# Two batches' adjacency patterns in one 32-bit word: a dilation ranked pair by pair in a two-layer graph network

## The chip, the cores and the metric

The kernel runs on one core of a Trainium2 chip. The metric is the device time of one execution in microseconds (us), from the first to the last instruction. The engines are named as in the profile: PE is TensorE's matmul, PEld its weight load, DVE is VectorE, ACT is ScalarE, POOL is GpSimd, and SP is the engine that issues most of the DMAs.

## The reference

The input is 16 graphs (batches) of 1024 nodes with 128 features (`x`), a weighted adjacency matrix `adj` of 1024 x 1024 for each (a fraction of about 0.06 of it is above zero, the pattern is symmetric), and a node mask of ones. Two layers are computed:

```
# layer 0
h = relu(layernorm(x))
three times:  h = h @ W + b;  nh = h / |h|;  h = (adj * (nh @ nh.T)) @ h     (relu after the last)
x = x + h
# layer 1
h = relu(layernorm(x))
keep = dilate(adj > 0)
three times:  agg = (adj * keep) @ h / degree;  out = agg @ Wr + h @ Wx + b
              h = batchnorm(relu(out / |out|))
x = x + concat(h1, h2, h3) @ Wl + bl
```

The dilation is the part that the change touches. It works on the true/false pattern of one batch, and it goes row by row, since what earlier rows remove is missing in later ones:

```
for n in range(1024):
    row  = pattern[n];  num = sum(row)
    sf   = (num + 1) // 2  if num > 10  else 1
    rank = cumsum(row)
    rm   = row & (rank % sf == 0)            # only where num > 1 and the mask is set
    pattern[n] = row & ~rm
    pattern[:, n] &= ~rm                     # the same entries in the column
```

So a row with more than 10 entries loses the entry of rank `sf`, and where `num` is even also the last one. For this, the rank of every entry in the row as it then stands is needed.

## The kernel before

Nodes lie in 8 chunks of 128, so that a 128 x 128 block of the adjacency is one tile. Layer 0 and the dilation don't depend on one another, and the kernel lays them side by side; layer 1 begins when both are done.

**Layer 0** (`layer0`, `Batch`) goes over 48 steps, 16 batches by 3 convolutions, two batches at a time in turn. In a step each of the 8 row chunks gets its products `pg` of normalised features (PE, L344), which DVE multiplies with the adjacency out of PSUM into `ew` (L353, L356). `pg` has two PSUM buffers. PE then turns part of `ew` (L373), ACT brings that back (`ew`, L374), and the sums go to `po` (L384, L398), which ACT evicts at the end of the step (`hTo`, L407). The sums of a row chunk are issued three chunks after its products. Some steps also turn a batch's adjacency on PE (`pt_a`, L260, evicted to `adjA`).

**The dilation** (`dilation`, `dilate`) goes over 16 blocks: 8 row chunks by 2 halves of 8 batches. The 128 nodes of a row chunk lie on the partitions. Of a block three generators are made.

- `loads()`, for each of 8 batches: 128 rows of the adjacency (`an`) are loaded by SP, ACT makes the pattern of ones and zeros in f16 with Sign and Relu (L587, L588; Relu counts the entries into `rest`), and DVE writes the part to the left of the diagonal block, times what was kept there by earlier rows (L594, with the count in `left`). That part comes through a transposing DMA from `keep_d`. After every fourth batch, PE transposes the four diagonal blocks (L608), ACT evicts them (`dT`, L610), and three matmuls each (L614 to L616) give `T`, the rank of every entry of the diagonal block counted from the row's middle (evicted by ACT, L618).
- `rounds()`: within a row chunk the rows depend on one another, and that is solved by iteration: 2 to 6 rounds of a guess `E` for the removed entries (DVE, L667) and its count on PE (`pc`, L673). Then `fin` holds, for each row, where the removed ranks lie.
- `scans()`: the removed entries of the diagonal block are subtracted from the pattern (DVE, L732). Then, for each of 8 batches, one running sum over the row of 1024 gives twice the rank, less one, of every entry (DVE, L741, `rank`); ACT takes the distance from the row's middle (Abs, L751); DVE compares with the radius (`kp`, L762), and POOL's queue stores `kp` to `keep_d` (L763).

The patterns of all blocks live in a ring `patt` of 10 slots; the pattern of batch `i` in a block is slot `(at0 + i) % SLOTS`. The next block's loads are taken one after each scan of the block before.

Where the rounds don't settle, where a row has 10 entries or fewer, or where a zero turns up that mustn't, a counter `astray` is raised, and a general loop (`dilation(exact=True)`, under `tc.If`) does the whole dilation again row by row.

**Order.** `dilation()` yields weights, an estimate of how much time a piece takes. After each piece, steps of layer 0 are issued until their share of the work has caught up:

```
total = 2 * (NCH * (BH * (0.75 + 3.3) + 0.4 + 2.5) + sum(ROUNDS) * 1.0)
for weight in dilation():
    done += weight
    while at * total < done * SPREAD * total0 and step0():
        pass
```

with `SPREAD` 0.93. Within this the framework's scheduler may place instructions of an engine a little earlier or later by priority; `tc.keep_in_program_order` holds the scans and the Abs in their order.

Of the kernel before, what the change touches and what calls it, by code (L numbers as in the profile page):

```python
# [8 lines left out]
F32 = mybir.dt.float32  # L9
F16 = mybir.dt.float16  # L10
I32 = mybir.dt.int32
AF = mybir.ActivationFunctionType
ALU = mybir.AluOpType
PSUM = bass.MemoryType.PSUM
# [2 lines left out]
P = 128  # L17
# [3 lines left out]
EVENS = 16777216.0  # L21

NEVER = -4096.0

LOW = 20.0

# [2 lines left out]
ROUNDS = (2, 2, 4, 6, 6, 3, 2, 6)  # L29
# [17 lines left out]
def tile_adj_preln_d2(  # L47
# [40 lines left out]
    nc = tc.nc  # L88
    B, N, D = x.shape
    NCH = N // P  # L90
# [4 lines left out]
    GT = 4  # L95
# [26 lines left out]
    ident16 = const.tile([P, P], F16, name="ident16")  # L122
# [36 lines left out]

    def transposed(psum_pool, dst, src, nm, func=AF.Copy, halves=range(NHALF)):  # L160

# [38 lines left out]
    with ExitStack() as actx:  # L200
        dctx = ExitStack()
        poold = dctx.enter_context(tc.tile_pool(name="ad", bufs=2, side="right"))
# [14 lines left out]
        off = pool1.tile([P, P], F16, name="off")  # L217
        after = pool1.tile([P, P], F16, name="after")
        for fill, value, op in ((0.0, -2.0, ALU.is_ge), (4.0 * FAR, 2.0 * FAR, ALU.is_gt)):
# [4 lines left out]
                up, up, pattern=[[1, P]], compare_op=op, fill=fill, base=0, channel_multiplier=-1  # L224
# [303 lines left out]

        BH = B // 2
        SLOTS = BH + 2  # L530
        patt = poold.tile([P, SLOTS, N + 2], F16, bufs=1, name="patt")
        nc.gpsimd.memset(patt[:, :, 0:2], 0.0)

        astray = poold.tile([P, BH], F32, bufs=1, name="astray")
        nc.vector.memset(astray, 0.0)
# [27 lines left out]
        def dilate(k, half, exact):  # L563

            nk = f"{'e' if exact else ''}{k}_{half}"
            cols = slice(k * P, (k + 1) * P)
            diag = slice(2 + k * P, 2 + (k + 1) * P)
            at0 = (2 * k + half) * BH

            def pattern(i):  # L570
                return patt[:, (at0 + i) % SLOTS, :]

            left = poold.tile([P, BH], F32, tag="left", name=f"left{nk}")
            rest = poold.tile([P, BH], F32, tag="rest", name=f"rest{nk}")
            if k == 0:
                nc.vector.memset(left, 0.0)
            rbias = poold.tile([P, BH], F32, tag="rbias", name=f"rbias{nk}")
            T = poold.tile([P, BH, P], F16, tag="T", name=f"T{nk}")
            E = radius = shift = low = None

            def loads():
                for i in range(BH):
                    b = half * BH + i
                    an = poold.tile([P, N], F32, tag="an", name=f"an{nk}_{i}")
                    nc.sync.dma_start(an, adj[b, cols, :])
                    on = pattern(i)[:, 2 + k * P :]
# [16 lines left out]
                    if i % GT == GT - 1:  # L603
                        four = range(i - GT + 1, i + 1)
                        bs_ = slice(i - GT + 1, i + 1)
                        pdt = ps_sm.tile([P, GT, P], F16, tag="sm", name=f"pdt{nk}_{i}")
                        for n, ii in enumerate(four):
                            nc.tensor.transpose(pdt[:, n, :], pattern(ii)[:, diag], ident16)  # L608
                        dT = poold.tile([P, GT, P], F16, tag="dT", bufs=1, name=f"dT{nk}_{i}")
                        nc.scalar.activation(dT, pdt, AF.Copy)  # L610
                        nc.vector.tensor_scalar(rbias[:, bs_], rest[:, bs_], 2.0, -2.0, ALU.mult, ALU.add)
                        pT = ps_sm.tile([P, GT, P], F32, tag="sm", name=f"pT{nk}_{i}")
                        for n, ii in enumerate(four):
                            nc.tensor.matmul(pT[:, n, :], lhsT=dT[:, n, :], rhs=upto, start=True, stop=False)  # L614
                            nc.tensor.matmul(pT[:, n, :], lhsT=pattern(ii)[:, diag], rhs=off, start=False, stop=False)
                            nc.tensor.matmul(pT[:, n, :], lhsT=ident16, rhs=after, start=False, stop=True)  # L616
                        for n, ii in enumerate(four):
                            nc.scalar.activation(T[:, ii, :], pT[:, n, :], AF.Identity, bias=rbias[:, ii : ii + 1])  # L618
                    yield 0.8

            def rounds():
                nonlocal E, radius, shift, low

                x0 = poold.tile([P, BH], F32, tag="x0", name=f"x0{nk}")
                nc.vector.scalar_tensor_tensor(x0, left, -0.5, rest, ALU.add, ALU.add)
                nc.vector.tensor_tensor(x0, x0, mbias[:, half * BH : (half + 1) * BH, k], ALU.add)
# [10 lines left out]
                E = poold.tile([P, BH, P], F16, tag="E", name=f"E{nk}")  # L637
# [87 lines left out]
            def scans():  # L725

                i = 0
                while i < BH:
                    at_ = (at0 + i) % SLOTS
                    n = min(BH - i, SLOTS - at_)  # L730
                    here = patt[:, at_ : at_ + n, diag]
                    nc.vector.tensor_tensor(here, here, E[:, i : i + n, :], ALU.subtract)  # L732
                    i += n
                ranks = {}
                for i in range(BH + 1):
                    if i < BH:

                        pt = pattern(i)
                        ranks[i] = rank = poold.tile([P, N], F16, tag="rank", bufs=3, name=f"rank{nk}_{i}")
                        tc.keep_in_program_order(  # L740
                            nc.vector.tensor_tensor_scan(rank, pt[:, 1 : N + 1], pt[:, 2:], 0.0, ALU.add, ALU.add)  # L741
                        )
                        yield True, 2.5
                    if i == 0:
                        continue

                    i -= 1
                    b = half * BH + i
                    pt, rank = pattern(i), ranks.pop(i)
                    tc.keep_in_program_order(  # L750
                        nc.scalar.activation(  # L751
                            rank, rank, AF.Abs, bias=shift[:, i : i + 1], scale=1.0 if exact else -1.0
                        )
                    )
                    kp = poold.tile([P, N], F16, tag="kp", name=f"kp{nk}_{i}")
                    if exact:
                        nc.vector.tensor_scalar(
                            kp, rank, low[:, i : i + 1], radius[:, i : i + 1], ALU.max, ALU.not_equal
                        )
                        nc.vector.tensor_tensor(kp, kp, pt[:, 2:], ALU.is_ge)  # L760
                    else:
                        nc.vector.tensor_scalar(kp, rank, radius[:, i : i + 1], None, ALU.not_equal)  # L762
                    nc.gpsimd.dma_start(keep_d[b][cols, :], kp)  # L763
                    yield False, 0.8

            return loads(), rounds(), scans()

# [71 lines left out]
    with ExitStack() as bctx:  # L839
# [135 lines left out]
        with kctx, ExitStack() as c1:  # L975
# [53 lines left out]
            for b in range(B):  # L1029
# [3 lines left out]
                now = Sums(0, b, hT, 3, 1, ps_a)  # L1033
# [76 lines left out]
        for l in (1, 2):  # L1110
            last = None
            then = start2(l, 0)
            for b in range(B):
                now, hT = then
# [23 lines left out]
            for h, pp, a in late:  # L1138
# [4 lines left out]
                for c in range(CPH):  # L1143
                    n = h * CPH + c
# [4 lines left out]
        for b in range(B):  # L1149
            y = pool2.tile([P, NCH, D], F32, tag=("o", "own")[b % 2], name=f"y_{b}")  # L1150
            for h, pp, a in project(2, b, normed(3, b, ab)):
                hc = slice(h * CPH, (h + 1) * CPH)

                if b % 2 == 0 and h == 1:
                    for c in range(CPH):
                        n = h * CPH + c
# [3 lines left out]
                for c in range(CPH):  # L1160
                    n = h * CPH + c
# [55 lines left out]
```

## Time and profile before

| | us |
|---|---|
| median of 3 runs | 2819.03 (2815.42 to 2820.99) |
| profiled execution, span | 2818.8 |
| PE busy | 2649.9 (94%) |
| DVE busy | 1947.1 (69%) |
| ACT busy | 1426.5 (51%) |
| POOL busy | 477.6 (17%) |
| 128 scans (L741) | 294.9, from 79.5 to 1511.1 us |

Busy time says how long an engine had an instruction in it; the matmuls overlap one another, and their ends are modelled. The page gives the span of the profiled execution and no other time for it. Layer 0 takes up to about 1640 us, the dilation ends at about 1515 us, and the convolutions of layer 1 take the rest. In a group's row there stand the line, the engine, the operation, what it writes and reads, the count, then busy us and mean ns of one, then the engine's idle time before these instructions and what ended it. In a row of waits there stand who waited for whom, the us in total, the times and the longest.

### The profile page before, as it was taken

The numbers are of one execution on the slowest core, as the hardware profiler recorded it, in microseconds if no ns is written. First come the engines' busy times: TensorE is split into PE (matmuls) and PEld (weight loads), VectorE is DVE, ScalarE is ACT, GpSimd is POOL, SyncE is SP. The second block draws the span as 40 slices with busy tenths as digits, with TensorE's granted clock in tenths as the row PEclk, the third lists the DMA queues.
The fourth block names the chain that finished last, engine by engine and source line by source line (L and its number), as shares of the span: only waits on it lengthen the run. The fifth ranks groups of instructions, "written<-read, shape, count | busy, mean of one in ns | idle before, by whom it ended". The sixth has DMA issues, their size and how long they took to land. (4 is left out here: it accounts for less than half of the span.)

```text
span 2818.8 us, 51980 instructions
## 1 busy us (share of the span) xinstructions
PE 2649.9 (94%) x18803; PEld 2193.2 (78%) x18803; DVE 1947.1 (69%) x4943; ACT 1426.5 (51%) x4097; POOL 477.6 (17%) x616
## 2 busy tenths in 40 slices
PE   6999999999999999999999999999989999999997
PEld 4666666676776676666676778888889999899997
DVE  3778778788888788889886467777762333456556
ACT  6757667558556566466454333343333334333334
POOL 3112112012012111121121012222220101010101
PEclk9999999999999999999999999999999999999999
DMA  8437347258366476386354069999976666576774
GB/s 283 135 128 241 99 159 240 75 159 245 85 201 173 101 226 186 95 254 182 93 178 162 1 234 386 402 402 387 402 297 214 203 216 201 188 238 228 234 237 135
DMA packets 382233, 585.22 MB, mean 208 GB/s; under 512 B 85200, under 2 KB 266448, under 8 KB 381968
## 3 DMA queue, kind: packets, MB, share of 16 engines
q1 hardware_dynamic: 343280, 425.28, 48.2%
q0 software_dynamic: 38688, 156.53, 14.8%
q8 instruction: 151, 2.47, 0.4%
q14 instruction: 114, 0.93, 0.1%
HBM read 403.44 MB, written 163.58 MB: 201 GB/s over the span
## 5 line engine op out<-in xcount | busy, mean ns | idle before, releaser
L890 PE MATMUL agg<-hw,aT 128*128 128x128 f32 (+1 forms) x6144 | 743.5, 277 | 8.2 <-DVE aT L995 7.3
L890 PEld LDWEIGHTS agg<-hw,aT 128*128 128x128 f32 x6144 | 713.4, 193 | 13.6 <-DVE aT L995 9.7
L344 PE MATMUL pg<-nhT 128*128 128x512 f32 (+3 forms) x1152 | 454.7, 497 | 40.4 <-DVE ew L356 39.1
L384 PE MATMUL po<-ew,hS 128*128 128x512 f32 (+3 forms) x1152 | 453.3, 497 | 8.1 <-ACT hTo L407 3.7
L356 DVE TENSOR_TENSOR ew<-pg,adjA 128x768 f32<-128x768 f32 (+3 forms) x528 | 423.6, 826 | 5.0 <-PE pg L344 5.0
L398 PEld LDWEIGHTS po<-ew,hS 128*128 128x128 f32 x2688 | 339.5, 193 | 39.1 <-issue 36.8
L398 PE MATMUL po<-ew,hS 128*128 128x128 f32 x2688 | 367.5, 277 | 1.2 <-ACT ew L374 1.2
L374 ACT ACTIVATE ew<-gt 128x512 f32<-128x512 f32 (+1 forms) x480 | 208.5, 464 | 245.3 <-PE gt L373 238.0
L741 DVE TENSOR_TENSOR_SCAN rank<-patt 128x1024 f16<-128x1024 f16 x128 | 294.9, 2305 | 0.1
L344 PEld LDWEIGHTS pg<-nhT 128*128 128x128 f32 x1152 | 187.9, 192 | 131.7 <-issue 89.3
L384 PEld LDWEIGHTS po<-ew,hS 128*128 128x128 f32 x1152 | 195.2, 193 | 99.8 <-issue 64.6
L373 PEld LDWEIGHTS gt<-ident,ew 128*128 128x128 f32 x1344 | 168.5, 143 | 100.7 <-issue 75.4
L373 PE MATMUL gt<-ident,ew 128*128 128x128 f32 x1344 | 212.3, 277 | 4.8 <-PEq L824 2.5
L948 POOL TENSOR_TENSOR o<-o,rn 128x512 f32<-128x512 f32 x93 | 108.5, 1167 | 638.3 <-DVE rn L942 627.6
L353 DVE TENSOR_TENSOR ew<-pg,adjA 128x128 f32<-128x128 f32 x384 | 108.1, 282 | 156.6 <-PE pg L344 117.3
L864 DVE TENSOR_TENSOR own<-pw,bs 128x256 f32<-128x256 f32 x192 | 81.4, 424 | 155.5 <-ACT hw L863 155.4
L862 PE MATMUL pw<-wrx,hT 128*128 128x256 f32 x768 | 179.7, 388 | 9.2 <-ACT hT L1065 8.4
L862 PEld LDWEIGHTS pw<-wrx,hT 128*128 128x128 f32 x768 | 145.1, 194 | 31.3 <-ACT hT L1065 9.2
L1013 ACT ACTIVATE aT<-pta 128x512 f32<-128x512 f32 (+3 forms) x160 | 71.3, 467 | 187.4 <-PE pta L1012 181.9
L751 ACT ACTIVATE rank<-rank,fin 128x1024 f16<-128x1024 f16 x128 | 146.7, 1151 | 36.3 <-DVE rank L741 35.6
L940 ACT ACTIVATE own<-o 128x128 f32<-128x128 f32 x378 | 112.7, 301 | 99.7 <-DVE o L919 99.5
L321 POOL TENSOR_TENSOR hS<-hN,rn 128x1024 f32<-128x1024 f32 x48 | 102.5, 2136 | 355.5 <-DVE rn L157 226.0
(169 smaller groups left out, 3930.6 us busy)
## 6 DMA issues: line engine op xcount, KB each, us to landing
an<-in_adj_dram SPq DMA_DIRECT2D x128, 512.0 KB, 4.3
keep<-kp POOLq DMA_DIRECT2D x128, 256.0 KB, 2.9
kb<-keep SPq DMA_DIRECT2D x128, 256.0 KB, 5.5
aT<-adT SPq DMA_DIRECT2D x32, 960.0 KB, 4.7
aT<-adT SPq DMA_DIRECT2D x32, 832.0 KB, 4.6
aT<-adT SPq DMA_DIRECT2D x32, 704.0 KB, 4.2
aT<-adT SPq DMA_DIRECT2D x32, 576.0 KB, 3.4
xb<-in_x_dram SPq DMA_DIRECT2D x31, 512.0 KB, 5.2
```

The costliest lines, as they stand in the source:

```text
L344: nc.tensor.matmul(pg[:, :n, :].rearrange("p c q -> p (c q)"), lhsT=self.nhT[:, q * P : (q + 1) * P], rhs=self.nhT[:, (q + c) * P : (q + c ...
L356: nc.vector.tensor_tensor(both[0][:, :, off, :], pg[:, own:n, :].unsqueeze(1).to_broadcast([P, 2, n - own, P]), both[1][:, :, off, :], ALU ...
L373: nc.tensor.transpose(pt[:, i, :], ew[:, at + i, :], ident)
L374: nc.scalar.activation(ew[:, at : at + n, :], pt[:, :n, :], AF.Copy)
L384: nc.tensor.matmul(self.po[:, c * P : (c + n) * P], lhsT=self.hS[:, q, :], rhs=ew[:, c - q : c - q + n, :].rearrange("p c q -> p (c q)"), ...
L398: nc.tensor.matmul(self.po[:, q * P : (q + 1) * P], lhsT=self.hS[:, q + n, :], rhs=ew[:, NCH - 1 - q + n, :], start=False, stop=closes and ...
L741: nc.vector.tensor_tensor_scan(rank, pt[:, 1 : N + 1], pt[:, 2:], 0.0, ALU.add, ALU.add)
L751: nc.scalar.activation(rank, rank, AF.Abs, bias=shift[:, i : i + 1], scale=1.0 if exact else -1.0)
L862: nc.tensor.matmul(pw[:, i, :], lhsT=hT[:, 2 * h + i, :], rhs=wrx[:, l, :], start=True, stop=True)
L890: nc.tensor.matmul(self.place(c), lhsT=aT[:, blk, :], rhs=self.hw[:, source, :], start=source == 0 and c % self.ga == 0, stop=ends(c, source),
L940: nc.scalar.activation(sq, o, AF.Square, accum_out=ss[:, c : c + 1])
L948: nc.gpsimd.tensor_tensor(self.o[:, hc, :], self.o[:, hc, :], rn.unsqueeze(2).to_broadcast([P, CPH, D]), ALU.mult)
```

## The change

Two batches share the ring's words. `patt` becomes 5 slots of 32-bit integers in place of 10 slots of f16, and `lanes` is the same memory seen as pairs of 16-bit integers: batch `i` and `i + 1` of a block are the low and the high half of a word. A running sum over the 32-bit words (L741's place) adds both halves at once, so a block has 4 scans in place of 8. [...]the high half may count up to 127 entries; `many` adds to `astray` where a row of a high half has more (`MOST`), and the general loop then does the work. That loop still scans each batch by itself.

What follows from the packing: Sign now works in place in `an`, and Relu writes the 16-bit lane; ACT copies the diagonal blocks of each pair into a dense f16 tile `dg`, of which PE takes every second element as weights; E is subtracted from a pair at a time; Abs reads one lane of `rank` and writes `kp`. `T` and `Z` have one buffer in place of two, `rank` has two (of 32 bits) in place of three (of 16), and `kp` three in place of two. Of a pair, first the scan is issued, then the two comparisons of the pair before; a load of the next block follows the scan and the first comparison. The weight of a batch in `total` falls from 3.3 to 2.05.

```diff
-        patt = poold.tile([P, SLOTS, N + 2], F16, bufs=1, name="patt")
-        nc.gpsimd.memset(patt[:, :, 0:2], 0.0)
+        patt = poold.tile([P, SLOTS // 2, N + 2], I32, bufs=1, name="patt")
+        nc.gpsimd.memset(patt[:, :, 0:2], 0)
+        lanes = patt.bitcast(I16).rearrange("p m (c l) -> p m c l", l=2)
...
+            def pair(i):
+                return (at0 + i) % SLOTS // 2
+
             def pattern(i):
-                return patt[:, (at0 + i) % SLOTS, :]
+                return lanes[:, pair(i), :, i % 2]
...
-            T = poold.tile([P, BH, P], F16, tag="T", name=f"T{nk}")
+            T = poold.tile([P, BH, P], F16, tag="T", bufs=1, name=f"T{nk}")
...
-                    nc.scalar.activation(on, an[:, k * P :], AF.Sign)
-                    nc.scalar.activation(on, on, AF.Relu, accum_out=rest[:, i : i + 1])
+                    right = an[:, k * P :]
+                    nc.scalar.activation(right, right, AF.Sign)
+                    nc.scalar.activation(on, right, AF.Relu, accum_out=rest[:, i : i + 1])
...
+                        dg = poold.tile([P, GT // 2, P, 2], F16, tag="dg", bufs=1, name=f"dg{nk}_{i}")
+                        for n in range(0, GT, 2):
+                            nc.scalar.activation(dg[:, n // 2, :, :], lanes[:, pair(four[n]), diag, :], AF.Copy)
                         pdt = ps_sm.tile([P, GT, P], F16, tag="sm", name=f"pdt{nk}_{i}")
-                        for n, ii in enumerate(four):
-                            nc.tensor.transpose(pdt[:, n, :], pattern(ii)[:, diag], ident16)
+                        for n in range(GT):
+                            nc.tensor.transpose(pdt[:, n, :], dg[:, n // 2, :, n % 2], ident16)
...
-                            nc.tensor.matmul(pT[:, n, :], lhsT=pattern(ii)[:, diag], rhs=off, start=False, stop=False)
+                            nc.tensor.matmul(
+                                pT[:, n, :], lhsT=dg[:, n // 2, :, n % 2], rhs=off, start=False, stop=False
+                            )
...
+                if not exact:
+                    many = astray[:, 1::2]
+                    nc.vector.scalar_tensor_tensor(many, x0[:, 1::2], MOST, many, ALU.is_gt, ALU.add)
...
-                Z = poold.tile([P, BH, P], F16, tag="Z", name=f"Z{nk}")
+                Z = poold.tile([P, BH, P], F16, tag="Z", bufs=1, name=f"Z{nk}")
...
-                    here = patt[:, at_ : at_ + n, diag]
-                    nc.vector.tensor_tensor(here, here, E[:, i : i + n, :], ALU.subtract)
+                    here = lanes[:, at_ : at_ + n, diag, :]
+                    gone = E[:, i : i + 2 * n, :].rearrange("p (m l) c -> p m c l", l=2)
+                    nc.vector.tensor_tensor(here, here, gone, ALU.subtract)
...
+                def ranked(i):
+                    rank = poold.tile([P, N], I32, tag="rank", bufs=2, name=f"rank{nk}_{i}")
+                    pt = pattern(i) if exact else patt[:, pair(i), :]
+                    tc.keep_in_program_order(
+                        nc.vector.tensor_tensor_scan(rank, pt[:, 1 : N + 1], pt[:, 2:], 0.0, ALU.add, ALU.add)
+                    )
+                    return rank.bitcast(I16).rearrange("p (c l) -> p c l", l=2)
+
+                def compared(i, rank):
                     b = half * BH + i
-                    pt, rank = pattern(i), ranks.pop(i)
+                    kp = poold.tile([P, N], F16, tag="kp", bufs=3, name=f"kp{nk}_{i}")
                     tc.keep_in_program_order(
                         nc.scalar.activation(
-                            rank, rank, AF.Abs, bias=shift[:, i : i + 1], scale=1.0 if exact else -1.0
+                            kp,
+                            rank[:, :, 0 if exact else i % 2],
+                            AF.Abs,
+                            bias=shift[:, i : i + 1],
+                            scale=1.0 if exact else -1.0,
                         )
                     )
...
-                        nc.vector.tensor_scalar(kp, rank, radius[:, i : i + 1], None, ALU.not_equal)
+                        nc.vector.tensor_scalar(kp, kp, radius[:, i : i + 1], None, ALU.not_equal)
                     nc.gpsimd.dma_start(keep_d[b][cols, :], kp)
...
+                was = None
+                for i in range(0, BH + 2, 2):
+                    now = None
+                    if i < BH:
+                        now = ranked(i)
+                        yield 1, 2.5
+                    for j in range(2):
+                        if was is not None:
+                            compared(i - 2 + j, was)
+                        yield int(i < BH and j == 0), 0.8 if was is not None else 0.0
+                    was = now
...
-        total = 2 * (NCH * (BH * (0.75 + 3.3) + 0.4 + 2.5) + sum(ROUNDS) * 1.0)
+        total = 2 * (NCH * (BH * (0.75 + 2.05) + 0.4 + 2.5) + sum(ROUNDS) * 1.0)
```

More of the change, by code (lines that the diff above doesn't have):

```diff
@@ L11 @@
 I32 = mybir.dt.int32
+I16 = mybir.dt.int16
 AF = mybir.ActivationFunctionType
@@ L23 @@
 NEVER = -4096.0
+MOST = 127.0
 LOW = 20.0
@@ L728, in scans @@
                 while i < BH:
-                    at_ = (at0 + i) % SLOTS
-                    n = min(BH - i, SLOTS - at_)
-                    here = patt[:, at_ : at_ + n, diag]
-                    nc.vector.tensor_tensor(here, here, E[:, i : i + n, :], ALU.subtract)
[L733 to L747, printed above, removed]
+                    at_ = pair(i)
@@ new lines, in scans @@
+                    n = min(BH - i, SLOTS - 2 * at_) // 2
+                    here = lanes[:, at_ : at_ + n, diag, :]
+                    gone = E[:, i : i + 2 * n, :].rearrange("p (m l) c -> p m c l", l=2)
+                    nc.vector.tensor_tensor(here, here, gone, ALU.subtract)
+                    i += 2 * n
+                def ranked(i):
[5 more added lines that the diff above has]
+                    return rank.bitcast(I16).rearrange("p (c l) -> p c l", l=2)
@@ L753, in scans @@
                         )
                     )
-                    kp = poold.tile([P, N], F16, tag="kp", name=f"kp{nk}_{i}")
                     if exact:
                         nc.vector.tensor_scalar(
-                            kp, rank, low[:, i : i + 1], radius[:, i : i + 1], ALU.max, ALU.not_equal
+                            kp, kp, low[:, i : i + 1], radius[:, i : i + 1], ALU.max, ALU.not_equal
                         )
-                        nc.vector.tensor_tensor(kp, kp, pt[:, 2:], ALU.is_ge)
+                        nc.vector.tensor_tensor(kp, kp, pattern(i)[:, 2:], ALU.is_ge)
@@ L761, in scans @@
                     else:
-                        nc.vector.tensor_scalar(kp, rank, radius[:, i : i + 1], None, ALU.not_equal)
+                        nc.vector.tensor_scalar(kp, kp, radius[:, i : i + 1], None, ALU.not_equal)
                     nc.gpsimd.dma_start(keep_d[b][cols, :], kp)
-                    yield False, 0.8
+                if exact:
+                    for i in range(BH):
+                        compared(i, ranked(i))
+                        yield 0, 1.0
+                    return
```

## The prediction

> **What bounds the kernel now.** I read the page's head and its slices first, then a table by stage, then who waits for whom, then the groups of instructions.
>
> ```profile
> span 2818.8 us, 51980 instructions
> PE 2649.9 (94%) x18803; PEld 2193.2 (78%) x18803; DVE 1947.1 (69%) x4943; ACT 1426.5 (51%) x4097; POOL 477.6 (17%) x616
> PE   6999999999999999999999999999989999999997
> DVE  3778778788888788889886467777762333456556
> ```
>
> TensorE is busy nearly everywhere, and no slice shows it starved. The dilation is laid between the matmuls of layer 0, in the first 21 slices or so. The table by stage (us; PE, PEld, DVE, ACT, POOL busy; granted clock; DMA) splits that stage where the last scan ends:
>
> ```profile
> 70.00:1520.00 1450.00, 1368.47 (x8667) 999.17 (x8666) 1196.69 (x2817) 901.36 (x2401) 252.26 (x314) 0.99 0.55 161
> 1520.00:1640.00 120.00, 117.05 (x644) 84.60 (x643) 57.03 (x147) 38.40 (x121) 9.62 (x7) 0.99 0.19 65
> ```
>
> With dilation TensorE idles 1450.0 - 1368.5 = 81.5 us (5.6%), beside a VectorE that is 83% busy. Without it, TensorE idles 3.0 us of 120, of which 2.5 us is one gap. So whatever the change does to VectorE can give back some 80 us at most. The rest of the span, 1640 to 2819 us, holds no dilation.
>
> One rule of the Trainium skill would say otherwise. Its page "Trainium Kernel Development and Optimization", section Best Practices, says to judge the distance to the limit by the share of weight loads (PEld) and not by matmul busy time. PEld is at 999.2/1450 = 69% in the first row, and read alone that leaves up to 450 us to win. But it is at 84.6/120 = 71% in the second row too, where nothing holds TensorE up: the evictions of a layer's result (ACT hTo L407 in the timeline) start there at 1540.28, 1568.12, 1595.95 and 1623.79 us, an even 27.83 us apart. 70% weight load is this loop at full pace. I take the 80 us.
>
> What ends TensorE's waits from 70 to 1520 us:
>
> ```profile
> PE pg L344 <- DVE ew L356: 39.1, 37, 3.2
> PE pT L614 <- ACT dT L610: 5.5, 7, 1.4
> PE pw L293 <- ACT adjA L261: 4.2, 6, 0.9
> PE po L384 <- ACT hTo L407: 3.7, 6, 1.1
> PE pc L673 <- DVE E L667: 3.7, 9, 0.8
> ```
>
> Half of it is one wait: the product pg has two PSUM buffers, and VectorE has not yet read the older one. VectorE works in order, so the read comes late when something long stands ahead of it. The longest is the scan:
>
> ```profile
> L741 DVE TENSOR_TENSOR_SCAN rank<-patt 128x1024 f16<-128x1024 f16 x128 | 294.9, 2305 | 0.1
> L356 DVE TENSOR_TENSOR ew<-pg,adjA 128x768 f32<-128x768 f32 x257 | 240.3, 947 | 3.3 <-PE pg L344 3.3
> L667 DVE TENSOR_TENSOR E<-T,mid 128x1024 f16<-128x1024 f16 x61 | 74.4, 1220 | 0.7
> L762 DVE TENSOR_SCALAR kp<-rank,fin 128x1024 f16<-128x1024 f16 x127 | 68.7, 547 | 55.5 <-ACT rank L751 55.1
> ```
>
> How much of the 81.5 us is the scans' doing? I went through TensorE's gaps in the timeline: 55.3 us of them lie under a scan or within 3 us after one. Those stretches cover about 128 x (2.3 + 3) = 678 us, so 8.2% of that time is idle; of the other 772 us, 26.2 us, or 3.4%. The difference, 4.8% of 678 us, is 32 us, or 0.25 us for each scan. The other 2.05 us of a scan is covered by work that TensorE has in hand.
>
> **The change, part by part.**
>
> *Scans.* One scan over 32-bit words ranks two batches: 64 in place of 128. No row shows an int32 scan. The nearest row is the f16 scan, 2305 ns for 1024 elements, [...]so that element width hardly sets it. The price lies between 2.3 us and twice that, if words of double width took double time. I take 2.3 us: VectorE loses 64 x 2.305 = 147.5 us of work. On TensorE's path: 64 x 0.25 = -16 us.
>
> *The subtraction of E (L732).* It takes 12.0 us in 25 instructions now, 691 ns for 1024. Afterwards E is read with a jump between neighbours. The Trainium skill's page "VectorE: DVE Perf Modes", section on Mode 2x_1P, speaks against this edit: two 16-bit elements a clock need step 1 in every operand. By L667, which reads a broadcast operand, 1024 elements take 1220 ns. So 12.0 x 1220/691 = 21.2, +9 us of VectorE; if the fast form were kept, 0. I take +9.
>
> *The count of rows above 127.* Sixteen more small operations; the like (L712) take 158 ns: +2.5 us of VectorE. x0 is a row's entries after earlier removals. The reference draws both directions at 0.03125, so about 64 of 1024 with a spread of about 8; 127 is eight spreads away, and the general loop isn't entered. Were it, the time would rise by far more than any range here.
>
> *Writing lanes.* Relu (L588) and the product with earlier removals (L594) write 16-bit values at every second place. Their inputs are 32 bits wide already (Relu's become so), and f32 and f16 rows of equal width run alike (L587 951 ns from f32, L588 953 ns from f16 at 896 elements), so I cost this at nothing. The upper end is double time on both, some 80 us on each engine; on VectorE that would eat over half of what the scans give. A lower end below nothing I exclude: the elements are as many.
>
> *Sign* now stays in an (L587's place), so it has no reason to wait for a scan any more; Relu has. ScalarE stands 93.5 us at L587 for the scan now, 73 times, with the turns of ew behind it; there will be 64 scans to wait for. TensorE's waits that end on ScalarE (dT, adjA, hTo: 13.4 us above) should lose about a quarter: -3 us.
>
> *Dense copies of the diagonal (dg).* Two for each four batches, 32 x 2 = 64 ScalarE copies of 128x256, 0.38 us each by L374 at that size: +24 us on an engine that is 62% busy. TensorE's transposes (L608) wait for them. Today L608 waits 0.1 us in all, and in the timeline it starts 5 to 15 us after its last Relu (679 to 688 us, 764 to 783 us). So the cover is the matmuls between; were it gone, 32 x 0.76 = +24 us. Some groups will be met late, as 7 of 32 are at dT: I take +2 us. Their weights are then read at every second element; L608's loads take 98 ns, an f32 load of 128 columns 193 ns. At the dearer one, 256 loads cost 24 us of PEld, which is 69% busy and mostly beside matmuls. I take 0.
>
> *Comparison.* Abs (L751) writes kp and not rank: the same 1151 ns on 1024 elements, read at every second place. kp's not_equal stays dense, 547 ns. ScalarE now waits for kp to be free, in three buffers, where VectorE waited with two. The keep DMAs on POOL's queue land in 2.9 us, in equal number, and nobody waits for one now. Rank has two buffers in place of three, but two words' worth each: the next scan stands behind two Abs of the pair before, which VectorE's own kp already waits for (55.1 us at L762, 36 times). Abs and kp come in twos now; I add nothing, but this is the new wait I trust least. T and Z with one buffer: both are read for the last time in the rounds, before the next block writes them. Queue SP issues the same loads.
>
> *Pacing.* The weights fall from 3.3 to 2.05 in the total and likewise in what is yielded, so dilation still ends at 0.93 of layer 0; a round gets more matmuls to hide behind.
>
> Sum on VectorE: -147.5 + 9 + 2.5 = -136 us, from 83% busy to 73%. Sum on the path: -16 - 3 + 2 = -17 us. The profiled span is 2818.8 us, 0.2 below the median of 2819.0, and the page shows nothing around it; so about 2802 us.
>
> **Rivals.**
>
> *1. VectorE's relief stays off the path.* For it: only 37 waits at pg stand against 128 scans. The gaps may just move, since pg's two buffers stay and E (1.2 us) and ew (0.95 us) still stand in a row. Against it: 8.2% against 3.4% idle. It gives 0 to -5 us: 2814 to 2819.
>
> *2. Slower: the 32-bit scan takes twice as long.* Place: L741. At 4.6 us VectorE's sum hardly falls, and each block outlasts what covers TensorE. If half of the 64 scans let 2.3 us more through, that is 32 x 2.3 = +74, less the 16 us saved: +58, 2877 us. It turns against the change at about 2.8 us a scan (half of 64 x 0.5 us is 16 us). Against it: the f16 row's pace is no width-bound pace.
>
> *3. Slower: copies and pairs in ScalarE's queue.* dg met by TensorE without cover (+24 us), or Abs of a pair held behind a turn that waits for TensorE (ACT ew waits 182.9 us there, up to 5.5 us at once). It needs over half of the 32 groups to be uncovered; it gives about +8 to +15 us, 2827 to 2834.
>
> *4. More than counted.* VectorE at 73% also shortens the 3.4% away from scans: a third of the 26 us and half of the 16 us left at scans, with the 16, give -33; pg's waits wholly gone (39) and ScalarE's 3 give -42: 2777 to 2786.
>
> **How the numbers follow.** Main case (2790 to 2812) 0.47; more than counted 0.15; no effect 0.15; ScalarE's queue and other small losses 0.16; dear scan or dear lane writes 0.07. What differs by less than 0.2% (5.6 us) can't be told from no change. Faster: 0.47 + 0.15 = 0.62; same 0.15; slower 0.23. The range, 2777 to 2832, leaves out the dear scan and the far ends. Cases of one sign hold most; within them, 2777 to 2812.
>
> **What would show it.** L741: 64 scans near 2.3 us. VectorE busy about 1060 us from 70 to 1520 us. PE pg <- DVE ew near 25 us in place of 39.1; the stage's TensorE idle time near 65 us. ACT's wait for the scan about halved. PE pdt L608 still waiting under 5 us. The stage from 1640 us on unchanged in length. I am wrong if scans take over 2.8 us, if L608 or a kp wait rises by tens of us, or if VectorE falls by 136 us and TensorE's idle time does not fall with it.

## The result, and the profile after

The changed kernel takes 2840.67 us (median of 4 runs, 2837.35 to 2844.69), against 2819.39 us before: a ratio of 1.0076 (95% interval 1.0062 to 1.0091), slower by 21 us. The range ended at 2832. (One execution of a later kernel, c2_lane_an3, took 5427 us; its ratio leaves that one out, and what happened in it isn't known.) The head of the page and two of its slice rows:

```profile
span 2835.6 us, 51969 instructions
PE 2640.7 (93%) x18803; PEld 2191.9 (77%) x18803; DVE 1835.2 (65%) x4895; ACT 1457.4 (51%) x4161; POOL 472.7 (17%) x616
PE   6889998998999999999999998999989999999997
DVE  3667767677778778778786466677772333456556
```

VectorE lost 112 us of work and the span grew by 17, at the same granted clock (0.985 over each of the two profiled spans). The table by stage (us; PE, PEld, DVE, ACT, POOL busy; clock; DMA) shows where:

```profile
70.00:1520.00 1450.00, 1346.34 (x8567) 988.36 (x8564) 1077.56 (x2754) 921.10 (x2445) 245.72 (x310) 0.99 0.54 160
1520.00:1640.00 120.00, 116.82 (x651) 84.31 (x651) 56.44 (x129) 42.19 (x127) 9.74 (x8) 1.00 0.19 68
```

VectorE is 74% busy there, as forecast (73%), but TensorE idles 103.7 us where it idled 81.5. The last eviction of layer 0 (hTo) begins at 1658.55 us in place of 1645.63: 13 of the 17 us. After it there are 1177.0 us against 1173.2; that part varies between 1173 and 1183 us over the profiles of this study, so I read nothing from it.

The scans did what they should (groups of 70 to 1520 us):

```profile
L756 DVE TENSOR_TENSOR_SCAN rank<-patt 128x1024 int32<-128x1024 int32 x64 | 147.5, 2306 | 0.1
L683 DVE TENSOR_TENSOR E<-T,mid 128x1024 f16<-128x1024 f16 x62 | 77.3, 1246 | 0.9
L778 DVE TENSOR_SCALAR kp<-kp,fin 128x1024 f16<-128x1024 f16 x124 | 72.2, 584 | 118.8 <-ACT kp L764 118.5
```

2306 ns for int32 against 2305 for f16. But VectorE now stands 118.5 us for ScalarE's Abs, twice what it did. What ends TensorE's waits tells the same:

```profile
PE pg L347 <- DVE ew L359: 31.6, 28, 4.7
PE po L387 <- ACT hTo L410: 16.1, 14, 3.6
PE pT L625 <- ACT dT L621: 15.2, 11, 2.6
PE pw L296 <- ACT hT L169: 6.6, 5, 2.1
PE px L421 <- ACT adjA L264: 5.4, 4, 3.0
```

The wait for VectorE fell from 39.1 to 31.6 us; the waits for ScalarE rose (hTo from 3.7 to 16.1, dT from 5.5 to 15.2). And ScalarE itself waits for something new:

```profile
ACT an L595 <- DMA an<-in_adj_dram: 136.4, 81, 5.2
ACT ew L377 <- PE gt L376: 129.0, 92, 4.9
ACT patt L596 <- DVE rank L756: 61.9, 40, 4.2
```

In the kernel before, Sign (L587 there) waited for the scan, and hardly for the load of `an`:

```profile
ACT patt L587 <- DVE rank L741: 93.5, 73, 2.9
ACT patt L587 <- DMA an<-in_adj_dram: 3.6, 3, 2.0
```

The 3.6 us have become 136.4. Half of the Signs started more than 12.7 us after their load had landed; now half start within 0.08 us of it (from the third block on, here and below). Some six microseconds of the timeline show what that does (start, us, engine, line):

```profile
183.18 0.83 PE L401 MATMUL po<-ew,hS 128*128 128x128 f32 x6
183.61 1.00 SPq L592 DMA_DIRECT2D an<-in_adj_dram  x2
...
183.93 0.20 ACT L596 ACTIVATION_READ_ACCUMULATOR patt<-an 128x1 f32 x1
...
187.48 0.95 ACT L595 ACTIVATE an<-an 128x896 f32<-128x896 f32 x1 [3.36 <-DMA an<-in_adj_dram]
188.34 1.01 ACT L410 ACTIVATE hTo<-po 128x1024 f32<-128x1024 f32 x1
...
189.49 2.90 PE L387 MATMUL po<-ew,hS 128*128 128x512 f32 x3 [3.62 <-ACT hTo L410]
```

TensorE has finished `po` at 184.01, and ScalarE is free at 184.13. But Sign is at the head of ScalarE's queue, and ScalarE stands idle for 3.36 us until the load lands. Only then come Sign and, behind it, the eviction hTo, for which TensorE idles 3.62 us. I followed all of TensorE's waits of this stage back in that way. Those that end on ScalarE are 61.2 us, where they were 23.2; and for 48.1 us of them ScalarE had come without a pause from a Sign that had stood for the load, where there was none before.

### The profile page after: what moved, and what is told of

The parts are those of the page before. It is cut to its first block, busy times and chain, and to the rows that moved or that the text cites. A ratio compares the mean times of both kernels' runs of the same rounds, so it can differ in the third digit from the quotient of the medians.

```text
span 2835.6 us, 51969 instructions
## 1 busy us (share of the span) xinstructions
PE 2640.7 (93%) x18803; PEld 2191.9 (77%) x18803; DVE 1835.2 (65%) x4895; ACT 1457.4 (51%) x4161; POOL 472.7 (17%) x616
## 5 line engine op out<-in xcount | busy, mean ns | idle before, releaser
L922 PEld LDWEIGHTS agg<-hw,aT 128*128 128x128 f32 x6144 | 713.6, 193 | 13.6 <-DVE aT L1027 9.7
L347 PE MATMUL pg<-nhT 128*128 128x512 f32 (+3 forms) x1152 | 451.2, 494 | 32.8 <-DVE ew L359 31.6
L387 PE MATMUL po<-ew,hS 128*128 128x512 f32 (+3 forms) x1152 | 449.8, 495 | 17.8 <-ACT hTo L410 16.1
L401 PE MATMUL po<-ew,hS 128*128 128x128 f32 x2688 | 361.4, 276 | 0.0
L1045 ACT ACTIVATE aT<-pta 128x512 f32<-128x512 f32 (+3 forms) x160 | 71.2, 466 | 188.5 <-PE pta L1044 170.2
L595 ACT ACTIVATE an<-an 128x1024 f32<-128x1024 f32 (+7 forms) x128 | 87.3, 685 | 154.8 <-DMA an<-in_adj_dram 142.2
L895 ACT ACTIVATE hw<-pw 128x256 f32<-128x256 f32 x192 | 73.8, 384 | 159.8 <-PE pw L894 156.1
```

The source lines that it names most:

```text
L347: nc.tensor.matmul(pg[:, :n, :].rearrange("p c q -> p (c q)"), lhsT=self.nhT[:, q * P : (q + 1) * P], rhs=self.nhT[:, (q + c) * P : (q + c ...
L387: nc.tensor.matmul(self.po[:, c * P : (c + n) * P], lhsT=self.hS[:, q, :], rhs=ew[:, c - q : c - q + n, :].rearrange("p c q -> p (c q)"), ...
L401: nc.tensor.matmul(self.po[:, q * P : (q + 1) * P], lhsT=self.hS[:, q + n, :], rhs=ew[:, NCH - 1 - q + n, :], start=False, stop=closes and ...
L922: nc.tensor.matmul(self.place(c), lhsT=aT[:, blk, :], rhs=self.hw[:, source, :], start=source == 0 and c % self.ga == 0, stop=ends(c, source),
```

## The experiments

Theory A: Sign's move into `an` is what costs. Sign wrote the ring before, and so was tied behind a scan that still read the ring. In `an` it is tied to the load alone, and is put early into ScalarE's queue. The rival, theory B: ScalarE simply has more work (copies, lane writes). Each ratio is to the kernel before, run on the same chip, with its 95% interval.

**Half the scans alone (b2_half_scans), on the kernel before.**

```diff
-                        ranks[i] = rank = poold.tile([P, N], F16, tag="rank", ...)
-                        tc.keep_in_program_order(nc.vector.tensor_tensor_scan(...))
+                        if exact or i % 2 == 0:
+                            ranks[i] = rank = poold.tile([P, N], F16, tag="rank", ...)
+                            tc.keep_in_program_order(nc.vector.tensor_tensor_scan(...))
+                        else:
+                            ranks[i] = ranks[i - 1]
...
```

The odd batches are compared with the even ones' ranks, so this kernel leaves out half of the ranking and keeps another pattern; so do the later kernels with half the scans.

> The kernel before with every second scan left out (the odd batch of a pair is compared with the even one's ranks, so the kept pattern is not the reference's; the counter for the general loop is cleared), Abs writing kp; one batch at a time as before, f16, all weights as before. Theory A (the scans' share of TensorE's gaps was rightly read, and something else ate it): 12 to 20 us faster than before, ratio 0.993 to 0.996. Theory B (VectorE's relief never reached TensorE): within 5 us of before, ratio 0.998 to 1.002.

2820.2 us, ratio 1.0002 (0.9990 to 1.0013). That looks like the verdict "VectorE's relief is worth nothing". But this run had the new wait too: the odd batches' slots, no longer read by a scan, left their Sign untied, and ScalarE stood 86.6 us for `an`, against 3.6. The last experiment comes back to it.

**Sign moved alone (b1_sign_in_an), on the kernel before.**

```diff
-                    nc.scalar.activation(on, an[:, k * P :], AF.Sign)
-                    nc.scalar.activation(on, on, AF.Relu, accum_out=rest[:, i : i + 1])
+                    right = an[:, k * P :]
+                    nc.scalar.activation(right, right, AF.Sign)
+                    nc.scalar.activation(on, right, AF.Relu, accum_out=rest[:, i : i + 1])
```

> The kernel before with the one edit that Sign works in place in an and Relu writes the f16 pattern from there. Theory A (Sign, no longer tied to the ring, is queued early on ScalarE and stands there for the load of an, with TensorE's evictions behind it): 12 to 25 us slower than before (1.004 to 1.009), ScalarE's wait for the DMA of an rising from 4 us to over 100. Theory B (extra ScalarE work, copies and lane writes, is what costs): within 4 us of before.

2877.97 us, ratio 1.0210 (1.0191 to 1.0229): 59 us slower with no more work on any engine, more than either theory allowed. Its profiled execution had a granted clock of 0.982 in place of 0.985; 0.3% of TensorE's 2650 busy us would be some 8 us of it (an estimate), so most is not the clock. ScalarE's waits:

```profile
ACT an L588 <- DMA an<-in_adj_dram: 134.8, 74, 5.9
ACT patt L589 <- DVE rank L742: 72.5, 58, 2.9
```

**Sign back in its lane (a1_sign_lane), on the changed kernel.**

```diff
-                    nc.scalar.activation(right, right, AF.Sign)
-                    nc.scalar.activation(on, right, AF.Relu, accum_out=rest[:, i : i + 1])
+                    nc.scalar.activation(on, right, AF.Sign)
+                    nc.scalar.activation(on, on, AF.Relu, accum_out=rest[:, i : i + 1])
```

> The changed kernel with Sign writing its 16-bit lane of the ring, as it wrote the ring before, and Relu working in place there. Theory A (Sign queued early on ScalarE): 15 to 30 us faster than the changed kernel, ratio to before 0.997 to 1.002; ScalarE's wait for the DMA of an falls to some us. Theory B (more work on ScalarE): no faster than the changed kernel, rather slower by the dearer write of Sign, ratio to before 1.007 to 1.011.

2796.61 us, ratio 0.9911 (0.9896 to 0.9926): 44 us faster than the changed kernel, more than theory A said, and faster than the kernel before. One operand turns a loss into a gain, though ScalarE has more to do (944 us from 70 to 1520 us, against 921). Theory B is out, and the clock is no rival: the two profiled executions were granted 0.986 and 0.985, and differ by 34 us. Its row by stage, and its waits:

```profile
70.00:1520.00 1450.00, 1378.76 (x8749) 1012.17 (x8748) 1095.85 (x2796) 944.15 (x2482) 249.91 (x315) 0.99 0.55 163
```

```profile
PE pg L347 <- DVE ew L359: 26.4, 27, 2.2
PE po L387 <- ACT hTo L410: 11.5, 11, 2.3
```

```profile
ACT patt L595 <- DVE rank L756: 71.2, 47, 4.2
ACT patt L595 <- DMA an<-in_adj_dram: 13.0, 9, 3.8
```

ScalarE still stands 71.2 us at Sign, for the scan now. By the time the scan is done the load has landed, and TensorE idles 71.2 us in place of 103.7. Only 3.3 us of that follow a Sign that stood for the load, in place of 48.1.

**Sign pinned to program order (a2_sign_pinned):** `tc.keep_in_program_order(nc.scalar.activation(right, right, AF.Sign))`.

> The changed kernel with Sign still in place in an, but held in program order on ScalarE. Theory A: as with Sign in its lane, 15 to 30 us faster than the changed kernel, ratio to before 0.996 to 1.002. Theory B (more work on ScalarE, or the pairs): no difference from the changed kernel, 1.006 to 1.009.

2832.83 us, ratio 1.0042 (1.0028 to 1.0055): between what the two theories said. ScalarE stands only 1.4 us for `an`. But Relu, which reads `an` last, now comes so late that the next load waits for it, and VectorE, which needs the same load, stands in its place (DVE's and SP's waits):

```profile
DVE patt L602 <- DMA an<-in_adj_dram: 85.4, 53, 4.3
```

```profile
SPq L592 <- ACT patt L596: 314.8, 75, 29.7
```

So two ways were open: (i) Sign's place in the queue, (ii) `an` held too long. Two runs were to part them.

**Sign in a tile of its own (s1_sign_own_tile):** `nc.scalar.activation(sg, right, AF.Sign)`, then Relu from `sg`.

> The changed kernel with Sign writing a tile of its own (f16, two buffers; E has one and kp two to make room), so that an is free as soon as Sign and the product with earlier removals have read it, and Sign is still not tied to the ring. Theory (i), the place in ScalarE's queue: still slow, ratio to before 1.004 or more, ScalarE standing over 80 us at Sign for the DMA of an. Theory (ii), an held until Relu: recovered, 0.990 to 0.997.

2848.48 us, ratio 1.0102 (1.0089 to 1.0116). Sign still starts 0.08 us after the landing, ScalarE still stands, and nothing is won. As a test of (ii) the run is weak: Relu no longer holds `an`, but VectorE's product reads it as late as before, so that it is freed 13.8 us after the landing (median), where the changed kernel took 13.6.

```profile
ACT sg L596 <- DMA an<-in_adj_dram: 125.2, 74, 4.3
```

**Sign in `an`, but behind the scan (s2_sign_behind_scan).**

```diff
-                    nc.scalar.activation(right, right, AF.Sign)
+                    first = nc.scalar.activation(on[:, 0:1], right[:, 0:1], AF.Relu)
+                    with tc.issue_after(first.ins):
+                        nc.scalar.activation(right, right, AF.Sign)
```

> The changed kernel with Sign in place in an, but queued behind a one-element write of the lane (128 more ScalarE instructions of some 0.2 us, 27 us in all), which waits for the scan as Relu does. Theory (i): recovered, 0.990 to 0.998, ScalarE's wait for the DMA of an under 40 us. Theory (ii): still slow, 1.004 or more, since an is held as long as in the changed kernel.

2795.86 us, ratio 0.9923 (0.9905 to 0.9941): recovered, with 128 more instructions on ScalarE and `an` held as long as in the changed kernel (13.3 us, median). The one element waits for the scan, and Sign stands behind it, and starts 9.8 us after the landing (median):

```profile
ACT patt L595 <- DVE rank L758: 72.2, 46, 4.2
ACT patt L595 <- DMA an<-in_adj_dram: 17.5, 10, 3.3
```

With `an` held alike and only Sign's place changed, the loss is gone: it is the place in the queue, (i). In the changed kernel as it stands, (ii) adds nothing that these runs show.

**A third buffer for `an` (c1_an3 on the changed kernel, c2_lane_an3 with Sign in its lane, c3_half_an3 on half the scans):** `tag="an", bufs=3`; room from `E` and `kp`, in c3 from `T` and `Z`.

> The changed kernel with a third buffer for an, so that its load can start a batch earlier; to make room, E has one buffer and kp two. Theory A (ScalarE's queue stands at Sign for a late load of an): ScalarE's wait for that DMA falls from 136 us to under 40, and the time by 15 us or more, ratio to before under 1.003. Theory C (it is Sign's place in the queue that hurts, whatever it waits for): under 8 us gained, ratio 1.005 to 1.009.

> Sign in its lane, and a third buffer for an (E one, kp two). Theory A: little is left to gain, since ScalarE waits 13 us for an there: within 6 us of the kernel with Sign in its lane, ratio to before 0.989 to 0.993. Theory D (loads are late everywhere, only less visibly): a further 8 us or more, ratio under 0.988.

> The kernel before with every second scan left out, as in the earlier run of half the scans (odd batches compared with the even one's ranks, counter cleared), and a third buffer for an (T and Z one). Theory A (half the scans would pay about 16 us, and the late load of an, 86.6 us of ScalarE's waits in that run, ate it): ratio to before 0.992 to 0.996. Theory B (VectorE's relief by itself is worth nothing): 0.998 to 1.002.

A miss: 2877.55 us, 1.0204 (1.0191 to 1.0218); 2802.75 us, 0.9942 (0.9929 to 0.9955); 2834.78 us, 1.0065 (1.0051 to 1.0079). All three are slower than without it, by 36, 9 and 18 us. The load did come earlier: in the first of the three `an` is freed 27.2 us after the landing (median) in place of 13.6. But Sign moved up with it. It still starts 0.08 us after the landing, and ScalarE stood 151.3 us for `an`. So an earlier load doesn't help a Sign that is tied to the load alone. Behind the early load, SP's queue now stands at the transposing load `kl` (L599), for VectorE and for stored `keep`:

```profile
SPq L599 <- DVE ew L359: 139.2, 33, 39.3
SPq L599 <- DMA keep<-kp: 124.0, 20, 16.6
SPq L599 <- DVE patt L602: 117.7, 19, 26.1
```

Why that run lost a further 36 us isn't settled. The buffers that `E` and `kp` gave up are not enough to tell it: s1_sign_own_tile gave up the same ones and stood 7 us behind the changed kernel.

**The pacing.** The lane kernel with the old weights (d1_old_pacing), and the kernel before with the new ones (g1_before_new_pacing):

```diff
-                        yield True, 2.5
+                        yield True, 1.25
...
-        total = 2 * (NCH * (BH * (0.75 + 3.3) + 0.4 + 2.5) + sum(ROUNDS) * 1.0)
+        total = 2 * (NCH * (BH * (0.75 + 2.05) + 0.4 + 2.5) + sum(ROUNDS) * 1.0)
```

(This is g1; d1 is the like in the other direction, 5.0 for a pair's scan and 3.3 in the total.)

> The changed kernel with Sign in its lane and the old pacing: a pair's scan yields 5.0 in place of 2.5, and the weight of a batch in the total is 3.3 again. Theory E (the gain of the kernel with Sign in its lane comes from giving the rounds a larger share of the matmuls): it loses 12 us or more of its 22, ratio to before 0.995 to 1.001. Theory A (it comes from half the scans): within 6 us of it, ratio 0.989 to 0.993.

> The kernel before with the changed kernel's pacing alone: a scan yields 1.25 in place of 2.5, and a batch's weight in the total is 2.05. Theory E (the rounds' larger share of the matmuls is what pays, with or without packing): ratio to before 0.991 to 0.996. Theory F (it pays only where the scans are halved; with 128 scans the same VectorE work in less TensorE time makes the gaps larger): 1.000 to 1.008.

d1: 2813.69 us, 0.9978 (0.9969 to 0.9987). g1: 2806.05 us, 0.9942 (0.9922 to 0.9961). The weights alone, with no packing at all, are worth 16 us, and the lane kernel loses 19 without them. By the evictions hTo in the timeline, g1 is ahead from the start: the third comes at 146.74 us in place of 151.34, the last at 1627.70 in place of 1645.63. The gain grows bit by bit; how it comes about isn't shown. TensorE idles as long from 70 to 1520 us as before (81.3 us, against 81.5), with 8706 matmuls in that time in place of 8667:

```profile
70.00:1520.00 1450.00, 1368.75 (x8706) 1003.54 (x8705) 1208.49 (x2831) 907.31 (x2405) 247.98 (x315) 0.99 0.55 162
```

A round of 1.5 in place of 1.0 (f1_rounds_more, on the lane kernel) goes too far:

> Sign in its lane, and a round weighs 1.5 in place of 1.0, in what it yields and in the total, so that still more matmuls of layer 0 lie beside the rounds. Theory E: a further 3 to 10 us, ratio to before 0.988 to 0.990. If the new pacing already balances the stage: within 3 us of the kernel with Sign in its lane or slower, 0.990 or more.

2818.70 us, 0.9992 (0.9983 to 1.0002).

**The copies (b3_dense_copies, on the kernel before; t2_copies_on_pool: in the lane kernel, on POOL).**

```diff
+                        for n in range(0, GT, 2):
+                            at_ = (at0 + four[n]) % SLOTS
+                            nc.scalar.activation(dg[:, n // 2, :, :], patt[:, at_ : at_ + 2, diag], AF.Copy)
...
```

(The transposes L608 and the matmuls L615 then read `dg`.)

> The kernel before with the dense copies of the diagonal blocks alone: 64 more ScalarE instructions of about 0.4 us, and TensorE's transposes and the off matmuls read them. The prediction's step: +2 us, ratio 0.999 to 1.002. If the copies are met by TensorE without cover: +12 to +24 us, 1.004 to 1.009.

> The changed kernel with Sign in its lane, and the dense copies of the diagonal blocks on POOL in place of ScalarE. The copies alone cost before 0.27%. If that is ScalarE's time: 4 us or more faster than with Sign in its lane, ratio under 0.9897. If POOL is slow or late with them, TensorE waits at the transposes: 0.992 or more.

b3: 2829.01 us, 1.0027 (1.0017 to 1.0036), about 8 us in place of the 2 predicted. No wait of TensorE tells where they go: the one at dT is 5.8 us, against 5.5. t2: 2802.8 us, 0.9939 (0.9921 to 0.9956), no better than on ScalarE.

**Loads spaced more evenly (d2_loads_spread, on the lane kernel):** `yield int(i < BH and j == 1), ...`

> Sign in its lane, and of a pair the next block's loads follow the scan and the second comparison, not the first, so that they are spaced more evenly. If the bunching of loads costs: 4 us or more faster than the kernel with Sign in its lane, ratio to before under 0.9895. If not, within 4 us of it: 0.9895 to 0.993. Slower if the load then meets the next scan at once.

2806.3 us, 0.9947 (0.9927 to 0.9968). The bunching of loads doesn't cost; spreading them does, by 10 us, and why isn't shown.

**Half the scans in the new order (s4_half_paired), and with the tie kept (t1_half_tied).** Both leave out every second scan of the kernel before, and have the changed kernel's pair order, pacing and numbers of buffers for `T`, `Z` and `kp`, without copies or lane writes. t1 adds one read:

```diff
                         now = ranked(i)
+                        tie = poold.tile([P, 1], F16, tag="tie", name=f"tie{nk}_{i}")
+                        tc.keep_in_program_order(nc.vector.tensor_copy(tie, pattern(i + 1)[:, N + 1 : N + 2]))
```

> The kernel before (f16 ring, Sign and Relu in the ring, no dense copies) with every second scan left out (odd batches compared with the even one's ranks, counter cleared), and with the changed kernel's pair order and pacing. Before with the new pacing alone gave 0.9942. If half the scans pay 12 to 20 us: 0.987 to 0.990. If VectorE's relief is worth nothing: 0.993 to 0.996. The difference to the kernel with Sign in its lane (0.9911) is what copies and lane writes cost.

> As the run with half the scans, pair order and new pacing (0.9931; odd batches compared with the even one's ranks, counter cleared), and VectorE reads one element of the odd batch's pattern after each scan, so that the next load of that slot is tied behind the scan as before. If half the scans are worth some 16 us and the untied Sign hid it: ratio to before 0.985 to 0.989, ScalarE's wait for the DMA of an under 30 us. If half the scans are worth nothing: 0.992 to 0.996.

s4: 2800.02 us, 0.9931 (0.9916 to 0.9945), the pacing's gain and hardly more. t1: 2789.03 us, 0.9887 (0.9869 to 0.9906). ScalarE's waits of s4, then of t1:

```profile
ACT patt L587 <- DMA an<-in_adj_dram: 93.1, 46, 5.5
ACT patt L587 <- DVE rank L738: 59.2, 44, 3.6
```

```profile
ACT patt L587 <- DMA an<-in_adj_dram: 13.7, 6, 4.8
ACT patt L587 <- DVE rank L738: 8.5, 7, 2.0
ACT patt L587 <- DVE tie L770: 57.3, 40, 3.6
```

ScalarE now stands for the tie in place of the load. With the tie, half the scans (and the pair order) are worth 0.9887 against g1's 0.9942, 15.5 us. Without it, the untied Sign of the odd batches takes 12 of them back.

## Why the prediction was wrong, by its steps

The runs line up from the kernel before to the changed one (1% is 28.2 us; each interval is about 0.15 to 0.2% to either side, so a difference of two holds to some 7 us, and the third step is no clearer than that):

| from | to | ratio | step, us |
|---|---|---|---|
| before | new pacing (g1) | 0.9942 | -16 |
| g1 | half the scans, tied (t1) | 0.9887 | -15.5 |
| t1 | packed, Sign in its lane (a1) | 0.9911 | +7 |
| a1 | Sign in `an`: the changed kernel | 1.0076 | +46.5 |

- *Scans, -16 us.* The size came out: 15.5 us, to some 7 either way, and 2306 ns an int32 scan. The dear scan (rival 2) is out. The way there was not the one told, so there is luck in the number. The prediction looked for the gain at pg's wait ("near 25 us in place of 39.1"). The new pacing alone takes that to 27.0 us with all 128 scans, and with half the scans it is 32.2 (g1, then t1):

```profile
PE pg L344 <- DVE ew L356: 27.0, 34, 2.4
PE pg L344 <- DVE ew L356: 32.2, 32, 2.7
```

TensorE's idle time in the stage does fall, from 81.3 to 68.2 us. By my count of its gaps, those under a scan or within 3 us after one fall from 51.3 to 20.7 us, and the others rise from 29.9 to 47.6. So what rival 1 said, that gaps may just move, holds for over half of them.
- *Sign, -3 us.* The step that failed. "It has no reason to wait for a scan any more" was seen and counted as a gain. What was late next wasn't asked: the load of `an`, 4.3 us from issue to landing. ScalarE had stood 3.6 us in all for it only because the scan ended later. Without the scan it stood 136.4 us, with TensorE's evictions behind it: +46.5 us in place of -3. The sign that the prediction named for being wrong is there too: VectorE has 119 us less to do from 70 to 1520 us, and TensorE's idle time there rose by 22 us.
- *Pacing.* Told ("a round gets more matmuls to hide behind") and costed at nothing, without a reason; it was worth -16 us. So the sum was short on both sides, and the kernel that the sum described, with Sign tied, ran at 2796.6 us.
- *Copies, +2 us.* Mis-sized: +8 alone. In the packed kernel copies and lane writes together are +7, which is within what the table can tell. The cover was misread, on the safe side: the Relu that ends at 679 us belongs to the next block, and at the two places named the transposes start 17.5 and 19.2 us after their last Relu, not 5 to 15. The other reading stands: TensorE waits 1.1 us at the transposes now.
- *Writing lanes, nothing.* Wrong on ScalarE: Relu took 96.0 us in place of 77.7 (120 and 119 of them, 70 to 1520 us), for the most part off the path, since the kernel with Sign in its lane pays this twice and is fast. On VectorE the product took 86.6 us in place of 85.5, close to nothing, as said.
- *Subtraction of E.* The dearer form came as taken: 1223 ns for 1024 elements (L749), against the 1220 taken and 691 before.
- *Comparison.* VectorE's wait for Abs, the one I trusted least, doubled (118.5 us). With Sign in its lane it is still 92.6 us and the kernel is fast; so alone it isn't what costs.
- *Rival 3* named the engine and the sign, but by copies without cover and by Abs behind a turn, at +8 to +15 us. The queue was blocked by a load.

The version that beats both is the changed kernel with Sign in its lane: 2796.6 us, 0.9911 (0.9896 to 0.9926). Sign in `an` behind the scan runs alike (0.9923).

## What to carry to other kernels

A wait on an in-order queue can be what keeps a worse one away. Before an edit unties an instruction, ask what it will stand for next, and who stands behind it; here 136 us of ScalarE at a load in place of a scan cost more than 64 scans saved. And cost a change of pacing by itself, on the old kernel: here it was worth 16 us, as much as half of the scans.

## What the runs showed of the hardware

ScalarE writing int16 values at every second place is slower than writing f16 densely: Relu over 128x896 takes 1217 ns in the lanes and 953 ns before, +28%. What it reads doesn't matter, f32 or f16 (b1, then the changed kernel, then s1):

```profile
L589 ACT ACTIVATE patt<-an 128x896 f16<-128x896 f32 x16 | 15.2, 949 | 12.0 <-DVE rank L742 12.0
L596 ACT ACTIVATE patt<-an 128x896 int16<-128x896 f32 x16 | 19.2, 1217 | 6.0 <-DVE rank L756 5.9
L597 ACT ACTIVATE patt<-sg 128x896 int16<-128x896 f16 x16 | 19.3, 1218 | 8.0 <-DVE rank L757 8.0
```

No run parts the type from the step. Reading int16 at every second place costs nothing (Abs over 1024: 1154 ns against 1151). A running sum over 1024 elements takes VectorE as long in int32 (2306 ns) as in f16 (2305).
